# Layer 1 of a two-layer transformer: values, queries and keys by seven products of half blocks, with the residual kept in DRAM

## The chip, the core and the metric

The kernel runs on one core of a Trainium2 chip. The metric is the device time of one execution in microseconds (us). The engines are TensorE (PE; PEld is its weight load), VectorE (DVE), ScalarE (ACT), GpSimd (POOL) and SyncE (SP), which here issues DMA transfers. Everything is computed in float32. SBUF is the core's working memory of 128 partitions; PSUM holds matmul results in banks of 128 x 512 float32.

## What is computed

The input is x, 4 sequences of 512 tokens with 512 features. Both layers add attention and a mixture of experts to x. Layer 0 (sparse and windowed attention with 16 heads of 128, then experts) is not touched. Layer 1, cut to what matters:

```
xn = layernorm(x)
q, k, v = xn @ wq.T + bq,  xn @ wk.T + bk,  xn @ wv.T + bv        # 16 heads of 32
attn = softmax(q k^T / sqrt(32)) v ;  attn_out = attn @ wo.T + bo
top2 of 8 experts by xn @ router ;  h_e = silu(xn @ We + be)
combined = sum over the token's two experts of gate * h_e
y = xn + combined @ proj + b ;  ffn_out = norm_w * y / rms(y)
out = x + attn_out + ffn_out
```

## The kernel before

**Layout.** `acc` holds the residual, 16 tiles of 128 tokens x 512 features, in SBUF through the whole kernel. `xnT` is the normalised input, transposed: 4 blocks of 128 features, 2048 tokens (512 per sequence b). `xnd` is the same input by rows, in DRAM. The weights of layer 1 (`wqT`, `wkT`, `wvT`, `woT`) are 4 blocks of 128 input features x 512.

**Layer 1, groups and steps.** Its work is 16 groups g = (b, j), a sequence b and a block j of four heads. A group has four key chunks kc, so there are 64 steps. A step computes the scores of one key chunk for four heads (`weights`, matmuls at L996, exponentials on ACT at L998), and the products of the step before with the values (`attend`, L1010), with the sums of the exponentials kept on VectorE (L1016). Around that, the loop places: at kc 0 and 1 the next group's queries and keys (`queries`, L985, 8 matmul instructions of 512 columns into one PSUM bank, evicted with its bias by VectorE at L987); at kc 2 one of the four token tiles of the next sequence's values (`values`, L975, evicted at L977 with the bias `wv_b`); at kc 1 to 3 the division by the sums of the group before (`sum_keys` L1024, `invert` L1034, `scale_context` L1041); at kc 3 one output tile (`output1`, L1056), which `add_part` (L1047) adds to `acc`. A tile of the residual gets two additions, one from attention and one from the experts, and is stored to `out` after the second.

**The jobs beside it.** `schedule(jobs1)` hangs the mixture of experts on the same steps: routing in steps 0 to 9; 39 expert tiles, tile i in step 13 + 3i/4 (`fetch` loads 128 token rows, L379, and the expert's weights, L381, through POOL into two buffers; `turn` transposes the rows, L388; `apply` multiplies, L398, and evicts with bias and silu, L400 to L406); from step 44 on `mix`, `turn_mix` and `project_mix` of the 16 token tiles (L1081 to L1107), the last of which ends in the second kind of `add_part`. The fetch of tile i+2 is given out in the step of tile i and needs tile i's buffer.

**The order.** The program is written in this order of steps; a scheduler then orders the instructions on each engine by its own estimate, within the dependences. Each engine works its list in order. SP's list holds the DMA issues of stores to `out`, to `xnd` and `yd`, and of plain loads. In layer 1 one PSUM tag, "mm", with three banks serves queries, values, outputs, experts, transposes and sums.

**Between the layers.** `next_layer(n)` normalises tile n of the residual, and then POOL adds the output bias of layer 1 to it (L814, `acc[:, n, :] + wo_b`). The last four tiles are done while layer 1 begins: the first values, then the first queries, around 1480 to 1505 us. The loads of `wqT`, `wkT`, `woT` and `wv_b` are issued by SP at 1476.6 to 1479.7.

Of the kernel before, what the change touches and what calls it, by code (L numbers as in the profile page):

```python
# [44 lines left out]
def two_layers(ctx: ExitStack, tc: tile.TileContext, a: dict, out: bass.AP, large: bass.AP):  # L45
# [72 lines left out]
    yds = [dram.tile([NS * P, HID], F32, tag=f"yd{i}", name=f"yd{i}") for i in range(2)]  # L118

# [688 lines left out]
    def next_layer(n, pool, bank):  # L808
        make_rows, turn_ = layernorm(n, pool, bank)

        def rows():
            make_rows()

            G.tensor_tensor(acc[:, n, :], acc[:, n, :], rout["wo_b"], ALU.add)  # L814
        return rows, turn_
# [153 lines left out]

    def values(b, t):  # L970
        if t == 0:
            v[b] = ap_.tile([P, TC, HID], F32, tag="v", name=f"v1_{b}")
        vp = bank1("mm", f"vp_{b}_{t}")
        for k in range(KC):
            PE.matmul(vp, lhsT=xnT[:, k, ds(b * S + t * P, P)], rhs=wa["wvT"][:, k, :],  # L975
                      start=(k == 0), stop=(k == KC - 1))
        V.tensor_tensor(v[b][:, t, :], vp, rows["wv_b"], ALU.add)  # L977

    def queries(g, i):
        b, j = groups1[g]  # L980
        if i == 0:
            qk[g] = ap_.tile([P, 2, S], F32, tag="qk", name=f"qk_{g}")
        qp_ = bank1("mm", f"qp_{g}_{i}")
# [3 lines left out]
        V.tensor_scalar(qk[g][:, i, :], qp_, qkb[:, i, j : j + 1], None, ALU.add)  # L987

# [55 lines left out]
    left = {n: 2 for n in range(NT)}  # L1044

    def add_part(n, part_):
        V.tensor_tensor(acc[:, n, :], acc[:, n, :], part_, ALU.add)  # L1047
        left[n] -= 1
        if left[n] == 0:
            nc.sync.dma_start(out=out_v[n], in_=acc[:, n, :])  # L1050

    def output1(b, t):
# [5 lines left out]
        add_part(n, op)  # L1058
# [27 lines left out]
    def turn_mix(n):  # L1086
        g0, x = held[n]
        tr = bank1("mm", f"trc_{n}")
        for f in range(KC):
            PE.transpose(tr[:, ts(f, P)], g0[:, ts(f, P)], ident)  # L1090
        cT_ = rout["mix"].tile([P, KC, P], F32, tag="xT", name=f"combT_{n}")
# [4 lines left out]
    def project_mix(n):  # L1096
# [11 lines left out]
        add_part(n, y)  # L1108
# [22 lines left out]
    for n in range(NT):  # L1131
        here = first + n
        for d, f in ((0, mix), (1, turn_mix), (2, project_mix)):
            jobs1.append((at[min(here + d, len(at) - 1)], lambda n=n, f=f: f(n)))
    run1 = schedule(jobs1)
# [21 lines left out]
    for g in range(NG):  # L1157
        b, j = groups1[g]
        for kc in range(TC):
# [16 lines left out]
            if kc == 2 and b + 1 < B:  # L1176
                values(b + 1, j)

            if kc == 3 and g > NJ:
                output1(*divmod(g - NJ - 1, TC))  # L1180
            run1((g, kc))
    attend(*late)
# [703 lines left out]
```

## Time and profile before

| | us |
|---|---|
| time, median of 3 runs (lowest to highest) | 2130.55 (2126.63 to 2132.97) |
| the profiled execution: its time | 2132.48 |
| its span, first to last instruction | 2130.7 |
| its mean granted TensorE clock | 0.993 |
| TensorE busy in the span | 2076.4 (97%) |
| layer 1, from the first matmul of the values to the end | 1479 to 2130.7 |
| queries and keys in layer 1 (L985) | 1499 to 2056 |
| values (L975) | 1479 to 1950 |
| expert tiles (L398) | 1587 to 1917 |
| L985, one matmul instruction of 512 columns, first to last of it | 0.593 (they overlap) |
| L977 and L400, 128 x 512 from PSUM on VectorE | 0.69 |
| L1016, 128 x 1024 on VectorE | 1.22 |
| L381, expert weights: issue on POOL | 1.22 |
| L381, issue to landing, lowest, median, highest | 6.6, 8.9, 10.3 |

All views are of one execution. Its first part is the totals: busy time, share of the span and instructions of each engine. A table by stage gives busy time and number of instructions of each engine in a stretch from A to B us, then the granted clock (1 is full speed), the share of time that the 16 DMA engines were busy, and GB/s. The waits list who waited on what: total us, times, longest. A timeline row has start, duration, engine, line, operation, result and operands, number of instructions, and in brackets the idle time before it and what ended it. "x8" on TensorE is one group of four float32 matmuls, two instructions each.

### The profile page before, as it was taken

The page shows a single profiled execution, that of the slowest core. Times are in us where ns is not written, and L with a number is a line of the kernel's source. Part 1 is how long each engine was busy: PE and PEld are TensorE (multiplying, and loading weights), DVE is VectorE, ACT ScalarE, POOL GpSimd, SP SyncE. Part 2 cuts the span into 40 slices and gives each one's busy share as a digit, 9 for nine tenths or more (in the row PEclk, how much of TensorE's full clock was granted, in tenths as well). Part 3 has the DMA queues.
Part 4 walks back from the last instruction along what each step waited for, and adds up shares of the span by engine and source line. Part 5 has one row for each costly group of instructions (what it writes and reads, how often), then busy time and mean ns, then how long its engine had stood idle before and what let it go on. Part 6 is the DMA issues. An engine that isn't in the chain of part 4 may idle for free.

```text
span 2130.7 us, 27241 instructions
## 1 busy us (share of the span) xinstructions
PE 2076.4 (97%) x8946; PEld 1197.8 (56%) x8946; DVE 1431.2 (67%) x3436; ACT 867.5 (41%) x2649; POOL 686.7 (32%) x667
## 2 busy tenths in 40 slices
PE   7999999999999999999999999999999999999998
PEld 4566666666666666666666666664334343433333
DVE  7878867666666666666676687785575444546775
ACT  3444444444444344444444444443243233323332
POOL 3322244343232333232333344443012222213440
PEclk9999999999999999999999999999999999999998
DMA  7101134323433432443332222212026666653321
GB/s 253 72 30 58 40 101 129 129 90 116 144 104 121 134 99 94 135 125 112 116 126 99 90 70 70 75 50 94 16 98 224 224 211 206 212 168 124 104 85 41
DMA packets 84917, 244.53 MB, mean 115 GB/s; under 512 B 11424, under 2 KB 23712, under 8 KB 74784
## 3 DMA queue, kind: packets, MB, share of 16 engines
q0 software_dynamic: 22592, 139.47, 19.7%
q1 hardware_dynamic: 61024, 101.13, 14.6%
q10 hardware_dynamic: 1152, 2.10, 0.3%
q8 instruction: 74, 1.21, 0.2%
q14 instruction: 75, 0.61, 0.1%
HBM read 205.44 MB, written 37.22 MB: 114 GB/s over the span
## 4 chain that ended last, share of the span: by engine, by line
PE 66%; issue 13%; DVE 9%; POOL 5%; ACT 3%; DMA 3%; SPq 0%; POOLq 0%; ACTq 0%; DVEq 0%
PE p L534 21%; PE op L701 10%; PE hp_r L398 7%; PE st L626 4%; PE qp L985 3%; PE sp L617 2%; POOL we_r L381 2%; PE o L1056 2%; PE st L996 2%; PE ca L670 2%; ACT sq L438 1%; DMA we_r<-in_ewx,wrow_r 1%; PE vp L975 1%; PE cx L1010 1%; PE trq L554 1%
## 5 line engine op out<-in xcount | busy, mean ns | idle before, releaser
L398 PE MATMUL hp_r<-we_r,xT_r 128*128 128x512 f32 x624 | 285.1, 600 | 4.7 <-DMA we_r<-in_ewx,wrow_r 4.6
L379 POOL DMA_INDIRECT xr_r<-xnd,rows_r x78 | 93.1, 1194 | 483.6 <-PE trm_r L388 414.2
L701 PE MATMUL op<-Wo,cT 128*128 128x512 f32 x512 | 230.2, 598 | 4.5 <-DVE lv L598 3.1
L634 POOL TENSOR_TENSOR lT<-lT,lmask 128x512 f32<-128x512 f32 (+1 forms) x128 | 156.2, 1232 | 181.8 <-ACT lT L630 181.6
L398 PEld LDWEIGHTS hp_r<-we_r,xT_r 128*128 128x128 f32 x624 | 116.0, 192 | 140.9 <-issue 130.6
L534 PE MATMUL p<-wB,x 128*128 128x384 f32 x512 | 176.4, 488 | 4.1 <-DVE u L590 3.4
L534 PE MATMUL p<-wT,x 128*128 128x384 f32 x512 | 178.4, 491 | 0.3 <-DVE wT L106 0.3
L534 PE MATMUL p<-wA,xnT 128*128 128x384 f32 x512 | 174.0, 491 | 0.4 <-DVE u L569 0.4
L701 PEld LDWEIGHTS op<-Wo,cT 128*128 128x128 f32 x512 | 92.2, 190 | 114.0 <-issue 77.4
L438 ACT ACTIVATE sq<-qb 128x128 f32<-128x128 f32 x384 | 119.0, 310 | 88.7 <-DVE qb L583 35.3
L998 ACT ACTIVATE pT<-st 128x1024 f32<-128x1024 f32 x128 | 123.8, 1018 | 56.8 <-PE st L996 46.0
L390 ACT COPY xT_r<-trm_r 128x512 f32<-128x512 f32 x78 | 45.3, 581 | 230.7 <-PE trm_r L388 173.1
L704 DVE TENSOR_TENSOR acc<-acc,op 128x512 f32<-128x512 f32 x128 | 87.7, 685 | 72.9 <-PE op L701 72.6
L534 PEld LDWEIGHTS p<-wB,x 128*128 128x128 f32 x512 | 94.1, 191 | 67.3 <-issue 9.6
L534 PEld LDWEIGHTS p<-wT,x 128*128 128x128 f32 x512 | 94.9, 193 | 62.4 <-issue 8.0
L534 PEld LDWEIGHTS p<-wA,xnT 128*128 128x128 f32 x512 | 95.5, 193 | 60.0 <-DVE u L569 1.6
L548 ACT ACTIVATE qb<-qb,ss 128x128 f32<-128x128 f32 x256 | 81.9, 390 | 111.6 <-POOL ss L440 109.6
L630 ACT ACTIVATE lT<-st,ss 128x256 f32<-128x256 f32 (+1 forms) x128 | 46.8, 448 | 177.8 <-PE st L626 176.5
L400 DVE TENSOR_TENSOR yr_r<-hp_r,we_r 128x512 f32<-128x512 f32 x78 | 53.7, 688 | 92.9 <-PE hp_r L398 92.9
L413 POOL DMA_INDIRECT row_r<-yd,slot_r x64 | 73.4, 1147 | 119.1 <-DVE row_r L1082 53.0
L626 PE MATMUL st<-qkT 128*128 128x256 f32 (+1 forms) x512 | 109.3, 354 | 0.0
L626 PEld LDWEIGHTS st<-qkT 128*128 128x128 f32 x512 | 92.2, 191 | 10.8 <-issue 1.0
(262 smaller groups left out, 4204.2 us busy)
## 6 DMA issues: line engine op xcount, KB each, us to landing
x<-xsd SPq DMA_DIRECT2D x112, 256.0 KB, 3.0
yd<-yr_r SPq DMA_DIRECT2D x78, 256.0 KB, 2.6
wA<-in_wA SPq DMA_DIRECT2D x16, 384.0 KB, 4.0
wB<-in_wB SPq DMA_DIRECT2D x16, 384.0 KB, 8.3
xnd<-xn SPq DMA_DIRECT2D x24, 256.0 KB, 2.0
acc<-in_x SPq DMA_DIRECT2D x16, 256.0 KB, 5.1
Wo<-in_Wo SPq DMA_DIRECT2D x8, 512.0 KB, 3.7
xsd<-x SPq DMA_DIRECT2D x16, 256.0 KB, 2.0
```

The lines of the kernel that those rows point to most:

```text
L379: G.indirect_dma_start(out=x, out_offset=None, in_=xnd, in_offset=at_rows(self.r.rows[:, i : i + 1]))
L398: PE.matmul(hp, lhsT=xT[:, k, :], rhs=w[:, ts(k, HID)], start=(k == 0), stop=(k == KC - 1))
L413: G.indirect_dma_start(out=x, out_offset=None, in_=self.yd, in_offset=at_rows(self.r.slot[:, k, n : n + 1]))
L438: A.activation(sq, x[:, h, :], AF.Square, accum_out=ss[:, h : h + 1])
L534: PE.matmul(p, lhsT=x[:, k, ts(c, P)], rhs=w[:, k, :], start=(k == 0), stop=(k == 1))
L548: A.activation(x[:, j, :], x[:, j, :], AF.Copy, scale=sq[t][:, j : j + 1])
L626: PE.matmul(st[:, ds((t % 2) * 256, n)], lhsT=qkT[:, HG + h, ts(t, P)], rhs=qkT[:, h, ds(t * P, n)], start=True, stop=True)
L634: G.tensor_tensor(dst, dst, lmask.rearrange("p a w j -> p (a w j)")[:, 0:n], ALU.mult)
L701: PE.matmul(op, lhsT=cT[:, h, ts(t, P)], rhs=wo[:, h, :], start=(h == 0), stop=(h == HG - 1))
L704: V.tensor_tensor(acc[:, n, :], acc[:, n, :], op, ALU.add)
L985: PE.matmul(qp_, lhsT=wa[("wqT", "wkT")[i]][:, k, ts(j, P)], rhs=xnT[:, k, ts(b, S)], start=(k == 0), stop=(k == KC - 1))
L998: A.activation(pt[:, ts(pair, 2), :], st, AF.Exp, scale=SCALE1)
```

## The change

**Seven products.** A product of two 2 x 2 block matrices takes eight block products, or seven with sums of blocks formed before and after. For sequences 1 to 3 the change computes two things in this way. Queries and keys of a group (`queries7`): the weight side is [wq; wk] against the two halves of the features, the right side the two halves of the features against the two halves of the sequence. At kc 0 the products 1, 2, 6, 7 and at kc 1 the products 5, 4, 3, each of 2 feature blocks with 256 columns, two products to a bank. Values of a sequence (`values7`): four products (1, 2, 6, 7) at kc 2 and three (4, 5, 3) at kc 3 of the last group of the sequence before, each of four matmuls of 256 columns. Sequence 0 is computed as before.

**Sums.** The weight sums (`sums_qk` 4 operations of 128 x 1024, `sums_v` 4 of 128 x 512 and one of 128 x 256) are formed once, the sums of xnT (`sums_right`, 4 of 128 x 512) for each of sequences 1 to 3, all on VectorE; some overwrite a block of `wkT`, `wvT` or `xnT`, the others and the intermediate results lie in `acc`. Products are put together by VectorE, 9 operations per sequence for the values, and 3 at kc 0 and 4 at kc 1 for a group's queries and keys, with one copy on ACT.

**The residual.** For that, `acc` is given up in layer 1: `next_layer` stores each tile to `accd` in DRAM (SP), `bring` loads a tile before an addition into a place in sequence 0's part of `xnT` (or, for the last sequence, in `acc`), `add_part` adds there, and after the first of a tile's two additions it is stored again unless the other addition is going to use the same place.

```diff
+    accd = dram.tile([T, HID], F32, tag="accd", name="accd")
...
             G.tensor_tensor(acc[:, n, :], acc[:, n, :], rout["wo_b"], ALU.add)
+            nc.sync.dma_start(out=accd[ts(n, P), :], in_=acc[:, n, :])
...
+    two = lambda x: x.rearrange("p (k t) -> p k t", k=2)
+    sq1, sq2, sq4 = (acc[:, ts(n, 2), :] for n in range(3))
+    sv1, sv2, sv4, tx1, tx2, tx4 = (two(acc[:, n, :]) for n in range(6, 12))
+    us = [acc[:, n, :] for n in range(12, 15)]
+    f1, f2 = slice(0, 2), slice(2, 4)
+    h1, h2 = slice(0, 256), slice(256, 512)
+    def sums_left(a11, a12, a21, a22, s1, s2, s4):
+        return [lambda: V.tensor_tensor(s1, a21, a22, ALU.add), lambda: V.tensor_tensor(s2, s1, a11, ALU.subtract),
+                lambda: V.tensor_tensor(s4, a12, s2, ALU.subtract), lambda: V.tensor_tensor(a21, a11, a21, ALU.subtract)]
+    def sums_qk():
+        wq, wk_ = wa["wqT"], wa["wkT"]
+        return sums_left(wq[:, f1, :], wq[:, f2, :], wk_[:, f1, :], wk_[:, f2, :], sq1, sq2, sq4)
+    def sums_v():
+        w = wa["wvT"]
+        for f in sums_left(w[:, f1, h1], w[:, f2, h1], w[:, f1, h2], w[:, f2, h2], sv1, sv2, sv4):
+            f()
+        V.tensor_tensor(rows["wv_b"][:, h2], rows["wv_b"][:, h2], rows["wv_b"][:, h1], ALU.subtract)
+    def block(b, f, half):
+        return xnT[:, f, ds(b * S + half * 256, 256)]
+    def sums_right(b):
+        b11, b12, b21, b22 = (block(b, f, t) for f in (f1, f2) for t in range(2))
+        V.tensor_tensor(tx1, b12, b11, ALU.subtract)
+        V.tensor_tensor(b12, b22, b12, ALU.subtract)
+        V.tensor_tensor(tx2, b22, tx1, ALU.subtract)
+        V.tensor_tensor(tx4, tx2, b21, ALU.subtract)
     def values(b, t):
         if t == 0:
             v[b] = ap_.tile([P, TC, HID], F32, tag="v", name=f"v1_{b}")
...
                       start=(k == 0), stop=(k == KC - 1))
         V.tensor_tensor(v[b][:, t, :], vp, rows["wv_b"], ALU.add)
 
+    def values7(b, part_):
+        w = wa["wvT"]
+        u1, u2, u3 = (two(u) for u in us)
+        bias = [rows["wv_b"][:, h].unsqueeze(1).to_broadcast([P, 2, 256]) for h in (h1, h2)]
+        def product(nm, left, right):
+            p = two(bank1("mm", f"v{nm}_{b}"))
+            for c in range(2):
+                for k in range(2):
+                    PE.matmul(p[:, c, :], lhsT=right[:, k, ts(c, P)], rhs=left[:, k, :], start=(k == 0), stop=(k == 1))
+            return p
+        if part_ == 0:
+            v[b] = ap_.tile([P, TC, HID], F32, tag="v", name=f"v1_{b}")
+            V.tensor_tensor(u1, product("p1", w[:, f1, h1], block(b, f1, 0)), bias[0], ALU.add)
+            V.tensor_tensor(v[b][:, 0:2, h1], product("p2", w[:, f2, h1], block(b, f2, 0)), u1, ALU.add)
+            V.tensor_tensor(u2, product("p6", sv2, tx2), u1, ALU.add)
+            V.tensor_tensor(u3, product("p7", w[:, f1, h2], block(b, f1, 1)), u2, ALU.add)
+            V.tensor_tensor(u3, u3, bias[1], ALU.add)
+        else:
+            V.tensor_tensor(v[b][:, 0:2, h2], u3, product("p4", w[:, f2, h2], tx4), ALU.subtract)
+            p5 = product("p5", sv1, tx1)
+            V.tensor_tensor(u2, p5, u2, ALU.add)
+            V.tensor_tensor(v[b][:, 2:4, h2], p5, u3, ALU.add)
+            V.tensor_tensor(v[b][:, 2:4, h1], product("p3", sv4, block(b, f2, 1)), u2, ALU.add)
     def queries(g, i):
         b, j = groups1[g]
         if i == 0:
             qk[g] = ap_.tile([P, 2, S], F32, tag="qk", name=f"qk_{g}")
+        if b:
+            return queries7(g, i)
         qp_ = bank1("mm", f"qp_{g}_{i}")
         for k in range(KC):
             PE.matmul(qp_, lhsT=wa[("wqT", "wkT")[i]][:, k, ts(j, P)], rhs=xnT[:, k, ts(b, S)],
                       start=(k == 0), stop=(k == KC - 1))
         V.tensor_scalar(qk[g][:, i, :], qp_, qkb[:, i, j : j + 1], None, ALU.add)
+    def queries7(g, part_):
+        b, j = groups1[g]
+        wq, wk_ = wa["wqT"], wa["wkT"]
+        u1, u2, u3 = (u[:, ts(g % 2, 256)] for u in us)
+        bq, bk = (qkb[:, n, j : j + 1] for n in range(2))
+        q, key = qk[g][:, 0, :], qk[g][:, 1, :]
+        def products(nm, *pairs):
+            p = bank1("mm", f"q{nm}_{g}")
+            for n, (left, right) in enumerate(pairs):
+                for k in range(2):
+                    PE.matmul(p[:, ts(n, 256)], lhsT=left[:, k, ts(j, P)], rhs=right[:, k, :], start=(k == 0), stop=(k == 1))
+            return p[:, h1], p[:, h2]
+        if part_ == 0:
+            p1, p2 = products("p12", (wq[:, f1, :], block(b, f1, 0)), (wq[:, f2, :], block(b, f2, 0)))
+            A.copy(u1, p1)
+            V.scalar_tensor_tensor(q[:, h1], p2, bq, u1, ALU.add, ALU.add)
+            p6, p7 = products("p67", (sq2, tx2), (wk_[:, f1, :], block(b, f1, 1)))
+            V.tensor_tensor(u2, p6, u1, ALU.add)
+            V.tensor_tensor(u3, p7, u2, ALU.add)
+        else:
+            p5, p4 = products("p54", (sq1, tx1), (wk_[:, f2, :], tx4))
+            V.tensor_tensor(u2, p5, u2, ALU.add)
+            V.scalar_tensor_tensor(key[:, h2], p5, bk, u3, ALU.add, ALU.add)
+            V.scalar_tensor_tensor(key[:, h1], u3, bk, p4, ALU.add, ALU.subtract)
+            p3, _ = products("p3", (sq4, block(b, f2, 1)))
+            V.scalar_tensor_tensor(q[:, h2], p3, bq, u2, ALU.add, ALU.add)
 
     def weights(g, kc):
 
...
         V.tensor_reduce(ends[:, 0, g : g + 1], rs, AX.X, ALU.max)
 
     left = {n: 2 for n in range(NT)}
-
-    def add_part(n, part_):
-        V.tensor_tensor(acc[:, n, :], acc[:, n, :], part_, ALU.add)
+    lies = {}
+    def bring(n, way):
+        if (n, 1 - way) in lies:
+            lies[n, way] = lies[n, 1 - way]
+            return
+        if n < NT - TC:
+            lies[n, way] = xnT[:, way * 2 + n % 2, 0:S]
+        elif left[n] == 2:
+            lies[n, 0] = lies[n, 1] = acc[:, 2 * NT - TC - 1 - n, :]
+        nc.sync.dma_start(out=lies[n, way], in_=accd[ts(n, P), :])
+    def add_part(n, part_, way):
+        x = lies.pop((n, way))
+        V.tensor_tensor(x, x, part_, ALU.add)
         left[n] -= 1
         if left[n] == 0:
-            nc.sync.dma_start(out=out_v[n], in_=acc[:, n, :])
+            nc.sync.dma_start(out=out_v[n], in_=x)
+        elif (n, 1 - way) not in lies:
+            nc.sync.dma_start(out=accd[ts(n, P), :], in_=x)
 
     def output1(b, t):
         n = b * TC + t
...
         for jj in range(NJ):
             PE.matmul(op, lhsT=cT1[b][:, jj, ts(t, P)], rhs=wa["woT"][:, jj, :],
                       start=(jj == 0), stop=(jj == NJ - 1))
-        add_part(n, op)
+        add_part(n, op, 0)
 
     r1 = Routing("r1", lg1, rp, const, bank1)
     held = {}
...
         tr = bank1("mm", f"trc_{n}")
         for f in range(KC):
             PE.transpose(tr[:, ts(f, P)], g0[:, ts(f, P)], ident)
+        bring(n, 1)
         cT_ = rout["mix"].tile([P, KC, P], F32, tag="xT", name=f"combT_{n}")
 
         A.activation(cT_, tr.rearrange("p (k t) -> p k t", k=KC), AF.Copy, scale=0.5)
...
         V.tensor_scalar(ss, ss, 1.0 / HID, 1e-6, ALU.mult, ALU.add)
         G.tensor_tensor(ss, ss, nhalf[:, 0:1], ALU.pow)
         V.scalar_tensor_tensor(y, y, ss[:, 0:1], rows["nw1"], ALU.mult, ALU.mult)
-        add_part(n, y)
+        add_part(n, y, 1)
 
 
     at = [(g, kc) for g in range(NG) for kc in range(TC)]
...
         here = first + n
         for d, f in ((0, mix), (1, turn_mix), (2, project_mix)):
             jobs1.append((at[min(here + d, len(at) - 1)], lambda n=n, f=f: f(n)))
+    left_ = sums_qk()
+    for place, f in (((1, 1), left_[0]), ((1, 2), left_[1]), ((1, 3), left_[2]), ((2, 0), sums_v), ((2, 1), left_[3])):
+        jobs1.append((place, f))
+    for b in range(1, B):
+        jobs1.append(((b * NJ - 2, 2), lambda b=b: sums_right(b)))
     run1 = schedule(jobs1)
 
     values(0, 0)
...
                     scale_context(g - 1)
             if kc < 2 and g + 1 < NG:
                 queries(g + 1, kc)
-            if kc == 2 and b + 1 < B:
-                values(b + 1, j)
-
+            if kc > 1 and j + 1 == NJ and b + 1 < B:
+                values7(b + 1, kc - 2)
+            if kc == 1 and g > NJ:
+                bring(g - NJ - 1, 0)
             if kc == 3 and g > NJ:
                 output1(*divmod(g - NJ - 1, TC))
             run1((g, kc))
+        if g + 1 == NG:
+            bring(NT - TC - 1, 0)
     attend(*late)
     sum_keys(NG - 1)
     output1(B - 2, TC - 1)
```

## The prediction

> **What bounds the kernel now.** The changed stretch is layer 1 of the profiled execution, 1479 us to the end at 2130.7. I read the page's totals first, then the table by stage, then the waits, and last the timelines of single steps. Totals:
>
> ```profile
> span 2130.7 us, 27241 instructions
> ...
> PE 2076.4 (97%) x8946; PEld 1197.8 (56%) x8946; DVE 1431.2 (67%) x3436; ACT 867.5 (41%) x2649; POOL 686.7 (32%) x667
> ```
>
> TensorE is the bound on the whole: whoever saves TensorE work saves time, unless TensorE then waits for something else. The table by stage (columns: PE, PEld, DVE, ACT, POOL busy; granted clock; DMA share; GB/s) tells where it would:
>
> ```profile
> 1516.00:1573.00 57.00, 56.83 (x299) 20.18 (x298) 52.00 (x109) 23.01 (x29) 4.42 (x4) 1.00 0.04 9
> 1600.00:1900.00 300.00, 295.87 (x1081) 121.19 (x1079) 137.52 (x170) 95.66 (x141) 74.89 (x69) 0.99 0.63 213
> 2000.00:2060.00 60.00, 57.06 (x226) 22.99 (x225) 42.32 (x58) 20.25 (x36) 27.78 (x26) 1.00 0.36 105
> 2050.00:2061.00 11.00, 10.80 (x41) 4.41 (x40) 10.51 (x13) 0.60 (x1) 4.25 (x3) 1.00 0.32 90
> 2060.00:2131.00 71.00, 59.35 (x204) 22.20 (x202) 40.38 (x62) 18.68 (x31) 8.93 (x9) 0.90 0.13 42
> ```
>
> Four regimes. From 1516 to 1573 VectorE is nearly as full as TensorE, 52 of 57 us (routing, sums over keys, reciprocals). In the 300 us of the experts TensorE stands 4.1 us in all, VectorE is under half busy and the DMA engines move 213 GB/s. In the mixing stage TensorE has 2.9 us of 60 free while VectorE fills single steps (2050 to 2061: 10.51 of 11), and in the tail 11.7 of 71. So in the expert stage TensorE looks like the sole bound. The waits in layer 1 (total, times, longest) and the landing times of the expert weights say that a second loop runs just beside it:
>
> ```profile
> POOL we_r L381 <- DVE yr_r L400: 65.0, 10, 9.0
> ...
> PE hp_r L398 <- DMA we_r<-in_ewx,wrow_r: 4.6, 4, 2.2
> ```
> ```profile
> DMA to landing us min/median/max: 6.6/8.9/10.3
> ```
>
> The weights have two buffers. POOL issues the load for expert i+2 only when VectorE has evicted expert i, and it lands 8.9 us later. One turn of that loop, on TensorE:
>
> ```profile
> 1677.14 3.60 PE L398 MATMUL hp_r<-we_r,xT_r 128*128 128x512 f32 x8
> ...
> 1683.61 3.70 PE L975 MATMUL vp<-wvT,xnT 128*128 128x512 f32 x8
> 1687.15 3.60 PE L398 MATMUL hp_r<-we_r,xT_r 128*128 128x512 f32 x8
> ...
> 1691.73 3.70 PE L398 MATMUL hp_r<-we_r,xT_r 128*128 128x512 f32 x8
> ```
> ```profile
> 1682.70 1.22 POOL L381 DMA_INDIRECT we_r<-in_ewx,wrow_r  x1 [0.30 <-issue]
> ```
>
> Expert 11's products end at 1680.7, its eviction at 1681.5, POOL issues the load of 13 at 1682.70, it lands at 1691.5, and 13 starts at 1691.73: TensorE's work between them (transposes 1.0, weights and attend 2.1, vp 3.5, expert 12's products 3.5, weights 1.1: 11.2) just fills the loop. The same stands before experts 5, 9, 17, 21, 25, 29, 33 and 37 (0.1 to 1.1 us between landing and start). Experts 18 and 34, whose landing the trace lacks, have 0.6 to 0.7 by their issue and 8.9. For most others the slack is 2 to 7 us. Work taken from TensorE inside such a turn comes back as a wait.
>
> **The change part by part.** A group of four 512-column matmuls (8 instructions) takes 3.54 us from start to start above (1683.61 to 1687.15), 3.43 where groups of one kind follow each other: 0.86 per matmul. In layer 0, 16 instructions of 384 columns took 5.17 us (L534), 0.32 each against 0.43: columns set the cost, and a half-block product (4 matmuls of 256) costs 1.72.
>
> **TensorE's own saving.** Queries and keys: 12 groups x (8 - 7) x 0.86 = 10.3 us, all at key chunk 1 (6 matmuls of 256, 2.58, for 3.43; chunk 0 stays 3.44). Values: 3 sequences x (4 x 3.43 - 7 x 1.72) = 5.1. Together 15.4 us, 0.7%. This is what the change can gain at most.
>
> **Values, moved.** I number the steps 4g + kc. Before, one vp of 3.5 us stood in steps 2, 6, 10, ..., 46. After, only the last group before each sequence has them: 4 products (6.87) in steps 14, 30, 46 and 3 (5.16) in 15, 31, 47. What leaving the others out is worth:
>
> Steps 2, 6, 10 (1524 to 1570) are VectorE-bound. VectorE loses three evictions (2.1 us) and gains one sum of weights that cannot be earlier (left_[3], 1.2; it overwrites wkT). Gain at least 2.1 - 1.2 = 0.9, at most the 57 - 51.1 = 5.9 to its busy time, of 10.6 removed. I take 3.
>
> Steps 22, 26, 34, 38 lie inside turns like the one shown (experts 11 to 13, 16 to 18, 27 to 29, 32 to 34). With vp gone from the turn above, TensorE comes to expert 13 at 1688.2 and its weights at 1691.5: 0.1 of 3.5 is left. The other turns have slack 0.6 to 0.7 and give that: 0.1 + 0.7 + 0.6 + 0.6 = 2.0 of 14.1. Bounds 0 and 14.1.
>
> Step 18 (a turn with slack) and step 42 (after the last expert) give 3.5 each, 7.0.
>
> Added are 3 x (6.87 - 3.53) + 3 x 5.16 = 25.5, of which 0.9 is absorbed by the wait before an expert of step 31: 24.6.
>
> Net 3 + 2.0 + 7.0 - 24.6 = -12.6 (a loss), between -17.6 (0.9 and 0 in the first two, nothing absorbed) and +2.4. The new sums of the products on VectorE (9 x 0.69 per sequence for 4 x 0.69) run in a stage where it is under half busy, beside the next product, with three banks to rotate; uncovered they would cost at most 3.4 per sequence. I count them below.
>
> **Queries.** Of the 12 savings of 0.86, eight fall at steps 13 to 41 and four at 45 to 57. In the first eight some are in turns without slack, and the expert's eviction in a chunk-1 step now stands behind four small additions: I take 4.9 of 6.9, bounds 0 and 6.9. In the last four VectorE sets the step:
>
> ```profile
> 2054.66 2.49 DVE L1016 TENSOR_TENSOR pS<-pT,pT 128x1024 f32<-128x1024 f32 x1
> 2057.08 0.94 DVE L1034 RECIPROCAL rsum<-rsum 128x128 f32<-128x128 f32 x1
> 2057.94 0.65 DVE L987 TENSOR_SCALAR qk<-qp,qkb 128x512 f32<-128x512 f32 x1
> 2058.51 1.75 DVE L1034 RECIPROCAL rsum<-rsum 128x128 f32<-128x128 f32 x2
> ```
>
> VectorE works without a gap from 2051.5 to 2062, and in such a step one 0.65 eviction becomes four of 128x256. No row has that size: 128x128 took 0.22 and 128x512 0.69, I take 0.42, so 1.7 for 0.65, +1.0 (bounds +0.2 and +2.1). Four steps of which some three are like this, less a little saved: -1.5, bounds -6 and +3.4. The ACT copy of p1 (0.31 to 0.58 by its rows) and three small additions at chunk 0 (+0.5) lie beside weights and attend: nothing; if that cover is gone, another 0.5 x 12.
>
> **The hand-over at 1480.** SP's queue and the first eviction of the values:
>
> ```profile
> 1478.13 0.43 SPq L776 DMA_DIRECT2D wkT<-in_wkT  x1
> 1478.61 1.03 SPq L776 DMA_DIRECT2D woT<-in_woT  x1
> 1479.69 0.68 SPq L72 DMA_DIRECT2D wv_b<-in_wv_b  x1
> ```
> ```profile
> 1489.25 1.29 DVE L977 TENSOR_TENSOR v<-vp,wv_b 128x512 f32<-128x512 f32 x2 [5.05 <-DMA wv_b<-in_wv_b]
> ```
>
> The twelfth store of the residual to DRAM is put before these loads on SP and waits for POOL's addition of wo_b (1477.8 to 1479.1): wkT, woT and wv_b go 1.4 to 2.1 us later. On VectorE three sums of query and key weights (3 x 1.16 by L1016) stand before the values' eviction: wkT at about 1487.3, sums to 1490.8, wv_b at 1491.2, eviction at about 1492 and not 1489.25. TensorE fills three banks and waits: -3, bounds -1 and -5. The other sums (4 x 0.69 of wvT and three times 4 x 0.69 of xnT) are issued before 1480, or in the under-half-busy expert stage: nothing, with the tail of layer 0 as cover (at most 1.4).
>
> **DRAM traffic.** 16 stores and some 30 loads and stores of 0.26 MB. The loads go out a group ahead, where a load of such rows (xnd to xa) landed in 2.8 us; but on SP the load of xa and the stores of y now stand behind stores that wait for additions, and POOL already waits 9.9 us for xa in 4 mixes. I take -2 for these and the exposed value sums, bounds 0 and -8.
>
> Sum: -12.6 + 4.9 - 1.5 - 3 - 2 = -14.2: 2132.5 + 14.2 = 2146.7 for the profiled execution (span 2130.7 and 1.8 around it). It lies 1.9 above the median of the runs shown, so **2144.8** is the forecast.
>
> One rule speaks against taking fillers out. Rows first: in the tail, with 11.7 us of 71 idle, the granted clock was 0.90; from 2000 to 2060, with 2.9 of 60 idle in pieces, 1.00. By these rows new waits of up to 3.4 us, scattered, leave the clock alone, and the sum above stands. The Trainium skill, TensorE: Matmul & The Clock Gate (Part 1: The HAM clock gate), says that the clock is halved once TensorE has been idle for a window of some 3.4 us. By it, as an estimate, four waits that just crossed that window would each run 3.4 us at half speed and lose 1.7, and the sum would be some 7 us worse.
>
> **The rivals.** Three.
>
> **Faster**, ending below 2124.2. TensorE stays the sole bound: expert weights land in time however little TensorE has to do. Then the values lose nothing in the four turns: +12.1, and 1516 to 1573 gives its 5.9: +2.9; queries 6.9: +2; the mixing steps hold (+3.5), hand-over -1: +2, traffic 0: +2. -14.2 + 24.5 = 10.3 gained, 2120.3. It decides when the loads take 5.4 us rather than 8.9; the fastest seen was 6.6. For it: TensorE 97% busy everywhere. Against: eight starts within 1.1 us of their landing. Chance 0.11.
>
> **The same**, 2124.2 to 2137.0. The loop gives way by half, the weights landing some 1.5 us sooner (7.4) in four turns: +6, and the hand-over costs 1 and not 3: +2. -6.2, 2136.8. 0.14.
>
> **Much slower.** In the mixing stage the loads of xa stand on SP behind stores whose additions come later on VectorE by the four additions of a chunk-1 step (1.7 to 2.2). If six of the 16 mixes are late by 2.2: 13 us more, 2158. For it: POOL's wait for xa and the gapless VectorE. Against: TensorE has other steps' work in hand. 0.10.
>
> My forecast has 0.65. That the change saves no TensorE work at all I leave out: fewer columns are multiplied, and columns set the cost.
>
> **How the numbers follow.** 0.3% of 2130.6, about what a measurement tells from no change, is 6.4. Faster 0.11, same 0.14, slower 0.65 + 0.10 = 0.75. The bad bounds of single terms give 2147 to 2151, two together up to 2156; the good bound of the values alone gives 2129.8, and rival 1 lies at 2120. The range 2129 to 2157 leaves out most of rival 1 (0.1) and of rival 3 (0.08). The forecast's own range is 2137 to 2155.
>
> **What the profile after would show.** Right: TensorE's busy time falls by some 15 us while the waits of hp_r for we_r grow from 4.6 to 12 us or more; 1516 to 1573 shrinks by 3 only; first v eviction near 1492; mixing steps no shorter. Wrong: waits for we_r as before (rival 1), the landing of we_r well under 8.9 (rival 2), or POOL waiting tens of us for xa (rival 3). The sum would be off most if the turns are not what holds steps 22, 26, 34 and 38.

## The result, and the profile after

The changed kernel takes 2143.42 us (median of 5 runs, 2141.29 to 2146.24) against 2129.48 before (also 5 runs, 2126.63 to 2132.97): a ratio of 1.0065, 95% interval 1.005 to 1.008. It is 13.9 us slower, although it multiplies fewer columns. The forecast was 2144.8, some 14 us slower. The profiled execution of the changed kernel stands 10.9 us above that of before (spans 2141.6 and 2130.7).

The totals on the page of the changed kernel:

```profile
span 2141.6 us, 27924 instructions
...
PE 2069.0 (97%) x9162; PEld 1239.1 (58%) x9162; DVE 1469.0 (69%) x3532; ACT 873.4 (41%) x2661; POOL 691.2 (32%) x667
```

TensorE is still busy for 97%. Its busy time fell by 7.4 us and not by 15; but busy time is no count of work (its ends are modelled, and a matmul at a lower clock is busy for longer): the kernel below whose values are only moved, with the same products as before, is busy for 2078.8, which is 2.4 us more. The timelines show the saving group by group.

The waits in layer 1 of the changed kernel (total, times, longest), and the landing times of the expert weights:

```profile
POOL we_r L383 <- DVE yr_r L402: 76.2, 12, 11.1
...
PE hp_r L400 <- DMA we_r<-in_ewx,wrow_r: 10.7, 7, 3.2
```
```profile
DMA to landing us min/median/max: 6.7/8.8/10.6
```

TensorE waits 10.7 us for expert weights where it waited 4.6, though they land as fast as before (8.8 against 8.9 us). This is the turn that the prediction showed, from expert 11 to expert 13, now without a group of the values in it; first TensorE, then POOL's issue:

```profile
1678.97 3.60 PE L400 MATMUL hp_r<-we_r,xT_r 128*128 128x512 f32 x8
...
1685.43 3.70 PE L400 MATMUL hp_r<-we_r,xT_r 128*128 128x512 f32 x8
1689.06 1.12 PE L1094 MATMUL st<-qk 32*128 32x512 f32 x2
1693.39 3.99 PE L400 MATMUL hp_r<-we_r,xT_r 128*128 128x512 f32 x5 [3.21 <-DMA we_r<-in_ewx,wrow_r]
```
```profile
1684.52 1.23 POOL L383 DMA_INDIRECT we_r<-in_ewx,wrow_r  x1 [0.30 <-DMA we_r<-in_ewx,wrow_r]
```

From the start of expert 11 to the start of expert 13 it was 14.59 us (1677.14 to 1691.73) and is 14.42 (1678.97 to 1693.39). 3.5 us of products left, and 3.21 came back as a wait in front of expert 13. (The view of TensorE ends at 1697, so its last row holds five of expert 13's eight instructions.) The reader should look at that row's bracket: the releaser is the DMA. Its issue at 1684.52 hangs on expert 11's eviction as before: the eviction ends at 1683.37 (1681.47 before), POOL issues the load of the token rows at 1683.27 (1681.45), and the weights follow 1.25 us behind in both. The bracket of POOL's row names another landing, that of expert 12 at 1684.27, but it is expert 11's buffer that the load fills.

The hand-over, on SP and on VectorE:

```profile
1480.30 0.32 SPq L817 DMA_DIRECT2D accd<-acc  x1
1480.67 0.48 SPq L778 DMA_DIRECT2D wkT<-in_wkT  x1
1481.20 0.67 SPq L778 DMA_DIRECT2D woT<-in_woT  x1
1481.91 0.74 SPq L72 DMA_DIRECT2D wv_b<-in_wv_b  x1
```
```profile
1487.34 1.23 DVE L985 TENSOR_TENSOR acc<-wkT 128x1024 f32<-128x1024 f32 x1 [0.76 <-DMA wkT<-in_wkT]
1488.60 1.23 DVE L985 TENSOR_TENSOR acc<-acc,wqT 128x1024 f32<-128x1024 f32 x1
1489.86 1.23 DVE L986 TENSOR_TENSOR acc<-wqT,acc 128x1024 f32<-128x1024 f32 x1
1491.35 1.29 DVE L1018 TENSOR_TENSOR v<-vp,wv_b 128x512 f32<-128x512 f32 x2 [0.27 <-DMA wv_b<-in_wv_b]
```

The store of the residual stands ahead of wkT, woT and wv_b on SP, whose issue is 2.2 to 2.6 us later than before, and three sums of weights stand ahead of the first eviction of the values, which starts at 1491.35 and not at 1489.25 (the forecast said 1492). But the first matmul of the values starts at 1480.31 here and at 1479.12 before, so 1.2 us of each of these differences stands ahead of layer 1.

For where the time goes I compare the start of each step in the two traces (the step's first exponential on ACT), the changed kernel less the one before:

| step | 0 | 3 | 8 | 12 | 16 | 19 | 24 | 28 | 32 | 40 | 43 | 48 | 63 | end |
|---|---|---|---|---|---|---|---|---|---|---|---|---|---|---|
| us | +1.2 | -2.3 | +0.8 | -2.5 | +7.7 | +3.4 | +3.2 | +1.1 | +8.4 | +5.7 | -1.3 | +11.8 | +12.0 | +11.0 |

The three clusters of the values (steps 14 to 15, 30 to 31, 46 to 47) put the time in; between them it comes back only in part. The +1.2 at step 0 is what stands ahead of layer 1: from the first matmul of the values to step 0 both traces take 30.59 us.

### The profile page after: what moved, and what is told of

Same layout as the page of the kernel before. It is cut to its first block, busy times and chain, and to the rows that moved or that the text cites. A ratio compares the mean times of both kernels' runs of the same rounds, so it can differ in the third digit from the quotient of the medians.

```text
span 2141.6 us, 27924 instructions
## 1 busy us (share of the span) xinstructions
PE 2069.0 (97%) x9162; PEld 1239.1 (58%) x9162; DVE 1469.0 (69%) x3532; ACT 873.4 (41%) x2661; POOL 691.2 (32%) x667
## 4 chain that ended last, share of the span: by engine, by line
PE 70%; DVE 12%; issue 6%; DMA 4%; ACT 4%; POOL 3%; SPq 0%; ACTq 0%; POOLq 0%; DVEq 0%
PE p L536 21%; PE hp_r L400 10%; PE op L703 10%; PE st L628 4%; PE sp L619 2%; DMA we_r<-in_ewx,wrow_r 2%; PE o L1170 2%; PE st L1094 2%; PE qp L1070 2%; DVE pS L1114 2%; ACT sq L440 2%; PE ca L672 2%; PE vp L1030 1%; PE trm_r L390 1%; PE cx L1108 1%
## 5 line engine op out<-in xcount | busy, mean ns | idle before, releaser
L400 PE MATMUL hp_r<-we_r,xT_r 128*128 128x512 f32 x624 | 285.5, 601 | 10.7 <-DMA we_r<-in_ewx,wrow_r 10.7
L1094 PE MATMUL st<-qk 32*128 32x512 f32 x512 | 96.0, 659 | 5.4 <-ACT pT L1096 5.3
```

Source lines behind the costliest of these rows:

```text
L400: PE.matmul(hp, lhsT=xT[:, k, :], rhs=w[:, ts(k, HID)], start=(k == 0), stop=(k == KC - 1))
L1094: PE.matmul(st[:, i, :], lhsT=qk[g][rows_, 1, ts(kc, P)], rhs=qk[g][rows_, 0, :], start=True, stop=True)
```

## The experiments

All ratios are against the kernel before, run beside them: its median was 2129.5 beside the change and 2130.0 to 2131.4 beside the others.

| kernel | us, median | ratio, 95% interval |
|---|---|---|
| the change | 2143.4 | 1.0065 (1.005 to 1.008) |
| values moved only | 2146.3 | 1.0081 (1.0063 to 1.0099) |
| values by seven products only | 2147.5 | 1.0090 (1.0073 to 1.0107) |
| queries and keys by seven products only | 2126.3 | 0.9981 (0.9972 to 0.9991) |
| the same for sequences 1 and 2 only | 2129.5 | 0.9992 (0.9983 to 1.0002) |
| residual in DRAM only | 2132.3 | 1.0011 (1.0001 to 1.0020) |
| values' seven products spread, sums in time | 2130.5 | 0.9998 (0.9989 to 1.0008) |
| residual in DRAM, three weight buffers | 2124.3 | 0.9968 (0.9958 to 0.9979) |
| values moved, three buffers | 2131.7 | 1.0005 (0.9995 to 1.0015) |
| values by seven products, three buffers | 2130.8 | 0.9997 (0.9987 to 1.0006) |
| queries by seven products, three buffers | 2117.2 | 0.9934 (0.9918 to 0.9951) |

### The place alone

```diff
-            if kc == 2 and b + 1 < B:
-                values(b + 1, j)
+            if kc > 1 and j + 1 == NJ and b + 1 < B:
+                for t in range(2):
+                    values(b + 1, 2 * kc - 4 + t)
```

> The kernel before with nothing changed but the place of the values of sequences 1 to 3: plain products, two token tiles at kc 2 and two at kc 3 of the last group of the sequence before, no sums, residual in SBUF. My theory (the place costs): the four fillers of 3.5 us per sequence go, of which some 13 us in all come back as shorter steps, and 3 x (3.4 + 6.9) - 0.9 = 30 us are added; about +16 us, 2145 against 2129.5. Rival (TensorE's work alone counts, so the place is indifferent, and products, sums or DRAM traffic make the change slow): within 3 us of before.

Measured: 2146.33, 15.6 us above before. No product, sum or DMA differs from the kernel before; only the place of nine groups does. It costs as much as the whole change (the intervals of the two overlap). In its trace TensorE's wait for the weights grows from 4.6 to 8.7 us:

```profile
PE hp_r L398 <- DMA we_r<-in_ewx,wrow_r: 8.7, 6, 3.5
```

### Queries and keys alone, values alone, the round trip alone

Queries and keys by seven products, values plain in their four places, in an order that the sums of xnT allow, and no sums of the values' weights:

```diff
-            if kc > 1 and j + 1 == NJ and b + 1 < B:
-                values7(b + 1, kc - 2)
+            if kc == 2 and b + 1 < B:
+                values(b + 1, (j + 2) % TC)
...
```

> The changed kernel with the values of sequences 1 to 3 as before (plain, one token tile at kc 2 of each group, in the order 2, 3, 0, 1 because the sums of xnT overwrite a block); queries and keys by seven products, residual in DRAM. My theory: the loss through the values goes (12.6 us), the rest stays: 2143.4 - 12.6 = 2131, between 2127 and 2132. Rival (seven products of queries or the DRAM traffic cost the time): 2138 or more.

Measured: 2126.27, 4.4 us faster than before. So the values carry the loss: without their change the kernel is 17 to 18 us faster than the changed one (17.15 between the medians, 17.0 between the spans, 18.4 if each is taken against the kernel before beside it), more than the 12.6 forecast.

Values by seven products, queries and keys plain (with one block of sums in a place of its own, so that xnT stays whole):

```diff
-        if b:
-            return queries7(g, i)
...
-        V.tensor_tensor(b12, b22, b12, ALU.subtract)
+        V.tensor_tensor(tx3, b22, b12, ALU.subtract)
...
```

> The changed kernel with plain queries and keys; values by seven products in the last group, residual in DRAM, sums of the values' weights and of xnT kept (one more place for a block of sums). My theory: 2129.5 + 12.6 + 1 to 3 for hand-over and traffic = 2143 to 2146, so about what the whole change costs. Rival (queries are the cost): 2132 or less.

Measured: 2147.46. It is 1.1 us from the plain values in the same places, within the intervals of the two: the saving of 5.1 us on TensorE left no mark in the total. (This kernel also keeps the residual in DRAM, which costs 1.6 by itself as the next run shows; that does not make up the 5.1.)

The round trip, with plain products everywhere and no sums:

```diff
-        if b:
-            return queries7(g, i)
...
-    left_ = sums_qk()
...
-    for b in range(1, B):
-        jobs1.append(((b * NJ - 2, 2), lambda b=b: sums_right(b)))
...
```

> The kernel before with the residual of layer 1 in DRAM (stores after POOL's addition, loads before each addition) and nothing else: no products, no sums. My theory: 1.2 us at the hand-over through the store ahead of the weights on SP, and up to 2 in the mixing stage: 2130 to 2133. Rival (the DRAM traffic on SP's queue makes the change slow): 2138 or more.

Measured: 2132.30, ratio 1.0011: 1.6 us above the median of before. 14.2 MB more (258.7 for 244.5) through the DMA engines and SP's queue are nearly free. Against this kernel the seven products of queries and keys gain 6.0 us (2126.3).

### A third buffer for the expert weights

In the kernels with the residual in DRAM, part of `acc` is free while the experts run. Every third expert tile is loaded there, so that the load of tile i+2 no longer waits for the eviction of tile i:

```diff
-            w = self.pool.tile([P, (KC + 1) * HID], F32, tag="we", name=f"we_{self.r.name}_{i}", bufs=bufs)
+            if self.silu and i % 3 == 2:
+                w = acc[:, 11:16, :].rearrange("p k t -> p (k t)")
+            else:
+                w = self.pool.tile([P, (KC + 1) * HID], F32, tag="we", name=f"we_{self.r.name}_{i}", bufs=bufs)
...
```

> The kernel before with the residual in DRAM as in the run of the round trip alone (2132.3), and a third buffer for the expert weights in the freed acc (every third expert tile), so that the load of tile i+2 no longer waits for the eviction of tile i. Base for the next runs. My theory: the waits of hp_r for we_r (4 us) go, 2127 to 2131. Rival (the weights' loads are bound by transfer, not by the buffer): unchanged, 2132, with the same waits.

Measured: 2124.29, 8.0 below the round trip alone, more than expected. The wait of TensorE for the weights is gone from the trace altogether, while they land as slowly as ever; here is the view of the tile of the weights:

```profile
DMA to landing us min/median/max: 6.8/9.1/10.2
```

So it was the buffer that bound the loads, not the transfer. Against the trace of the round trip alone step 19 is 4.6 us shorter: a wait of 2.90 us in front of expert 9 is gone, and with it a lowered clock behind it (see the clock, below). The same with the values moved:

> The same with plain values in the last group, two tiles at kc 2 and two at kc 3. With two buffers the move cost 15.6 us. My theory: of the 31 us of vacated products the loop over two buffers ate most of those in steps 22 to 38; with three buffers all six after step 17 come back (21) and some 5 of the three before: the move costs about 5, so 5 above the run with the third buffer alone. Rival (not the loop; the vacated steps are held by something else, or the added steps are dearer than their products): 13 to 16 above it.

Measured: 2131.67, 7.4 above the run with the third buffer alone, against 15.6 with two buffers. The step starts of the two traces show it: with three buffers the steps 18, 22, 26, 34 and 38 give 3.43 us back each and step 42 3.21. With two, steps 22 and 34 gave nothing (they lost 0.5 and 1.9 us) and 26 and 38 gave 2.5 and 2.9. With three buffers the added steps of the first two clusters cost their products and no more, 3.43 and 6.87. The loop is thereby shown to be what ate the vacated steps.

Values by seven products in those places:

> Values by seven products in the last group, plain queries and keys, residual in DRAM, three buffers for the expert weights. Plain values in the same places with three buffers took 2131.7. My theory: the vacated steps give their time back as there, and of the 5.1 us less on TensorE some stays, less 1 at the hand-over and some 4 in steps 46 to 48, where the trace of the changed kernel shows TensorE waiting for VectorE to free banks: 2129 to 2133. Rival (the loop was not the cause, values by seven products are slow in themselves): 2140 or more.

Measured: 2130.78. Without the loop the saving of the seven products is seen: against the plain values in the same places each of the first two clusters is 1.6 to 1.7 us shorter (1.72 by the sum). The third is not: from step 46 to 48 this trace loses 3.2 us. There TensorE waits 2.33 us for an eviction, and the clock is at 0.50 for 3.4 us behind it. The rest of the kernel loses 4.3 more in this trace, but it is that of the slowest of ten runs (2135.86); the medians differ by 0.9, in favour of the seven products and within the noise.

Queries and keys by seven products, plain values, three buffers:

> Queries and keys by seven products, plain values in their four places, residual in DRAM, three buffers for the expert weights. With two buffers 2126.3, and the trace gave none of the 6 us saved in steps 13 to 40. My theory: they come back, with the waits for we_r: 2117 to 2122. Rival (VectorE's additions hold those steps): 2125 to 2128.

Measured: 2117.19, ratio 0.9934: 14 us faster than before (10 to 17 by the interval), and the fastest of all kernels here. The table by stage, of the queries' kernel with two buffers and then with three (PE, PEld, DVE, ACT and POOL busy, clock, DMA share, GB/s):

```profile
1600.00:1900.00 300.00, 295.20 (x1162) 137.43 (x1161) 147.68 (x204) 98.35 (x148) 73.28 (x69) 0.99 0.66 224
```
```profile
1600.00:1900.00 300.00, 300.00 (x1204) 140.25 (x1203) 151.60 (x209) 101.90 (x154) 73.19 (x68) 1.00 0.66 225
```

TensorE stands 4.8 us of 300 in the first and never in the second, with the same traffic. By the step starts, the eight savings of the queries' seven products in steps 13 to 41 gained 0.5 us with two buffers (against the round trip alone), and 2.8 us with three (against the third buffer alone). That is not the whole 6.9: in steps 17, 21, 29 and 33 the 0.84 is seen each time and in step 41 0.77, but at steps 13, 25 and 37 the order of the expert tile against the queries shifts, so that the step is 4.73 us shorter and the next 5.13 longer, a loss of 0.4 each in place of a gain of 0.84. These eight are the same with two buffers; there step 31 is 2.1 us longer besides, where the wait for expert 25's weights is 1.43 us (1.00 in the round trip alone) and the clock is halved behind it. What makes the three dearer was not tried, nor was the whole change, values included, with three buffers.

### The values' products spread over four groups

Products 1 and 2 at kc 2 of the first group, 3 of the second, 6 and 7 of the third, 5 and 4 of the fourth:

```diff
-            if kc > 1 and j + 1 == NJ and b + 1 < B:
-                values7(b + 1, kc - 2)
+            if kc == 2 and b + 1 < B:
+                values7(b + 1, j)
...
```

> The changed kernel with the seven products of the values spread over kc 2 of the four groups: products 1 and 2; 3; 6 and 7; 5 and 4 (intermediate results in the tile of the values itself, 10 operations on VectorE for 9); two buffers for the weights. My theory: the place was the cost; with fillers back in every group it is near the run with plain values (2126.3), from 2123 to 2130. Rival (the products of the values themselves are dear: VectorE's operations, sums, banks): 2135 to 2143.

Measured: 2131.52. In this kernel product 3 of sequence 1 read the sums of the weights before they were formed, the work being the same. With the sums in time:

> As the run before with the values' products spread over kc 2 of four groups (1 and 2; 3; 6 and 7; 5 and 4), with the sums of the values' weights formed four steps earlier, before product 3 of sequence 1 uses them. There the time was 2131.5. My theory as it stands after that run: the place gives back most of the 17 us that the clustered values cost over plain ones, but with two weight buffers the saving of 5 us on TensorE does not come back and VectorE's additional operations cost a few: 2127 to 2132. Rival (the products themselves are as dear as their cluster): 2138 or more.

Measured: 2130.46, the same as before the change (0.9998). The same seven products, spread out, take 13 us less than in a cluster; so they are not dear in themselves. But with two buffers they are no gain either: plain values in one group each, at the same key chunk, took 2126.3.

### Which queries gain

> Queries and keys by seven products for sequences 1 and 2 alone, plain for sequence 3, whose queries lie in the mixing stage (steps 45 to 57); plain values in their places, residual in DRAM, two weight buffers. With sequence 3 as well it was 2126.3, with none 2132.3. By my prediction the seven products of sequence 3 lose 1.5 and this kernel takes some 2125. By the traces of those two runs (no gain in steps 13 to 40, several us after 45) it is sequence 3 that gains: 2129 to 2132.

```diff
-        if b:
+        if b in (1, 2):
             return queries7(g, i)
...
```

Measured: 2129.52, 3.2 above the kernel in which sequence 3 has seven products too (1 to 5 by the scatter of the runs). So sequence 3, whose queries lie in the mixing stage, gains some 3 us: my prediction, which had it lose 1.5, is wrong there. The step starts agree: from step 45 to 58 sequence 3's products gain 3.1 us in this pair of traces, 2.9 against the round trip alone, and 2.3 in the pair with three buffers.

## Why the prediction was right, point by point

The mechanism, that vacated steps do not come back beside a second loop while added ones cost their full price, is what the runs show. But the total (13.9 for 14.2) is closer than its parts, and that is luck: the values cost 17 and not 12.6, the queries gained 6.0 and not 3.4, the hand-over and the DRAM traffic cost some 2 and not 5. Of the signs I had named, the waits for the weights stopped at 10.7 (I said 12 or more), and TensorE's busy time fell by half of what I said.

The values' term by stretches, from the starts of the steps (the changed kernel less the one with seven products for queries only; plus is a loss):

| steps | 0 to 13 | 14, 15 | 16 to 29 | 30, 31 | 32 to 43 | 44 to 47 | 48 to end | sum |
|---|---|---|---|---|---|---|---|---|
| forecast, us | -3 | +8.5 | -4.3 | +7.6 | -4.7 | +8.5 | 0 | +12.6 |
| measured, us | -2.5 | +8.7 | -5.6 | +5.5 | -4.8 | +12.7 | +1.5 | +15.4 |

In steps 30 and 31 the queries' kernel itself has the 2.1 us of step 31 named above; against the kernel before, the stretch costs 7.8.

**The loop over the weights' two buffers: right in kind, and in two of four turns in size.** The prediction gave 2.0 of 14.1 us back in steps 22, 26, 34 and 38. The move alone, run with two and with three buffers (15.6 and 7.4 us), shows that the loop decides this. By the step starts of the changed kernel against the one with seven products for queries only, the four steps gave -1.4, +2.6, +0.1 and +2.5 us: 3.7 in all. Steps 26 and 38 gave more than the 0.6 to 0.7 that I read from issue and 8.9 us: expert 18's weights were issued at 1730.1 and its products began at 1737.04, so they landed within 6.9 us. That is the mechanism of the second rival, and it held in two of four turns.

**Steps 2, 6 and 10: right in size, in part by luck.** Forecast 3 us, of a bound of 5.9; up to step 13 the trace shows 2.5. But steps 2, 6 and 10 gave 8.4 us by themselves (3.4, 1.6 and 3.4), and 3.6 went again in step 7, over which the clock is halved, as shown below. The prediction had held VectorE alone responsible.

**The added steps: right for two clusters, too small for the third.** Steps 14 and 15 together grew by 8.65 us for 8.5. In that cluster the products run as priced, 1.73 us from start to start:

```profile
1609.66 1.99 PE L1030 MATMUL vp<-wvT,acc 128*128 128x256 f32 x8
1611.49 1.89 PE L1030 MATMUL vp<-acc 128*128 128x256 f32 x8
1613.22 1.89 PE L1030 MATMUL vp<-acc,xnT 128*128 128x256 f32 x8
1614.95 3.60 PE L400 MATMUL hp_r<-we_r,xT_r 128*128 128x512 f32 x8
```

The step that failed is "run in a stage where it is under half busy, beside the next product, with three banks to rotate". This holds in the expert stage, but the third cluster lies in steps 46 and 47, in the mixing stage. There, first TensorE and then VectorE:

```profile
1944.01 3.72 PE L1030 MATMUL vp<-wvT,xnT 128*128 128x256 f32 x16 [0.64 <-DVE qk L1083]
1947.57 1.89 PE L1030 MATMUL vp<-acc 128*128 128x256 f32 x8
1951.05 1.99 PE L1030 MATMUL vp<-wvT,xnT 128*128 128x256 f32 x8 [1.59 <-DVE acc L1034]
1952.88 3.60 PE L1215 MATMUL po<-pw,combT 128*128 128x512 f32 x8
```
```profile
1948.52 0.74 DVE L1196 SCALAR_TENSOR_TENSOR row_r<-row_r,gate_r,row_r 128x512 f32<-128x512 f32 x1
1949.18 1.21 DVE L1114 TENSOR_TENSOR pS<-pS,pT 128x1024 f32<-128x1024 f32 x1
1950.32 0.68 DVE L1034 TENSOR_TENSOR acc<-vp,wv_b 128x512 f32<-128x512 f32 x1
1950.92 0.93 DVE L1132 RECIPROCAL rsum<-rsum 128x128 f32<-128x128 f32 x1
1951.78 0.62 DVE L1035 TENSOR_TENSOR v<-vp,acc 128x512 f32<-128x512 f32 x1
```

Two products run at 1944.01, a third at 1947.57, and then the banks are full: VectorE is among the sums of the keys, the gates and the reciprocals, evicts the first product only at 1950.32, and TensorE waits 1.59 us. From step 44 to 48 the kernel lost 12.7 us against the one with plain values, for 8.5 priced; waits for banks, 0.64 and 1.59, make 2.2 of the 4.2. The two traces are 1.6 us apart at step 0 already, and little of that is the values': 1.3 stands at 300 us, in layer 0, where the two programs are the same. The sums of the values' weights do cost something: behind the first of them (1435.79 on VectorE) TensorE falls 0.5 us behind the trace of before, and in the kernel without these sums it does not. The prediction put them at nothing, with 1.4 as the bound.

**Queries: too little, and both parts wrong.** I gave 4.9 in the expert stage and -1.5 in the mixing stage, 3.4 in all. Measured against the round trip they gained 6.0: 0.5 up to step 41, and the rest behind it, some 3 of it through sequence 3. In the expert stage I gave 4.9 of 6.9; with three buffers 2.8 came, so the loop took 2.3, and the rest went into the three shifts of order named above, of which I had thought only as the eviction behind four additions. In the mixing stage "VectorE sets the step" was the step that failed. VectorE did get its additional work (in 2000 to 2060 it was busy 45.9 us with seven products for sequence 3 and 42.4 without), and still the kernel gained. My reading, which no run tests by itself, is that a gapless VectorE in an 11 us stretch isn't yet the bound of the stage: the same 60 us hold steps where it has room, and the 0.86 saved on TensorE counts there. Here are the two table rows, first without and then with seven products for sequence 3 (the 0.97 of the first holds a stretch of 3.4 us at half the clock; the second trace has its own just ahead of the window, at 1996.6, and from step 45 to 58 each has one, so the clock does not make the gain):

```profile
2000.00:2060.00 60.00, 57.04 (x222) 22.76 (x221) 42.43 (x60) 19.71 (x34) 28.03 (x25) 0.97 0.46 140
```
```profile
2000.00:2060.00 60.00, 58.10 (x265) 27.76 (x267) 45.93 (x75) 21.83 (x39) 27.96 (x24) 1.00 0.49 149
```

**Hand-over and DRAM: too dear.** I gave 3 and 2. Counted from the first matmul of the values the first eviction is 0.9 us later and step 0 not at all (30.59 us in both traces). "TensorE fills three banks and waits" is what failed: in both traces it runs two groups of the values, the router's products (3.6 us), a transpose and a third group in the same time, and none of them waits for the eviction. The 1.2 us at step 0 come from layer 0: 0.5 stands there from 100 us on, where the programs are the same, and 0.5 comes with the sums named above. The round trip in all costs 1.6. My third rival, loads of xa held up on SP, did not come in its size: POOL's wait for xa rose from 9.9 us to 16.1, and to 14.3 in the kernel with the round trip alone.

**The rivals.** "Faster" fell for the reason that was held against it, and its condition could be made: with loads that need not wait for an eviction, the kernel with seven products for the queries ends at 2117. Its sum had a slip: with the mixing steps at +3.4 in place of -1.5 the term is 4.9 and not 3.5, and its time 2118.9. "The same" was right on two turns of four.

## The clock

The rule weighed in the prediction turned out to matter, and my reading of the rows, that waits of up to 3.4 us leave the clock alone, was wrong. The changed kernel around step 7 (TensorE busy, its granted clock, DMA share, GB/s), and TensorE's timeline there:

```profile
1540.00:1545.00 5.00, 3.66 (x27) 1.00 0.02 3
1545.00:1550.00 5.00, 4.27 (x16) 0.64 0.00 0
1550.00:1555.00 5.00, 5.00 (x30) 0.67 0.00 2
1555.00:1560.00 5.00, 5.00 (x31) 1.00 0.00 0
```
```profile
1542.21 1.07 PE L1108 MATMUL cx<-pT,v 128*32 128x512 f32 x8
1543.21 0.46 PE L359 MATMUL tp_r<-mark_i_r,mark_r_r 128*128 128x78 bf16 x8
1545.73 2.99 PE L1094 MATMUL st<-qk 32*128 32x512 f32 x8 [2.07 <-ACT pT L1096]
1548.65 1.94 PE L1108 MATMUL cx<-pT,v 128*32 128x512 f32 x8
```

Behind a wait of 2.07 us the granted clock is 0.50 for 6.8 us, from 1546.4 to 1553.3 (the 0.64 and 0.67 above are means over 5 us), and eight score matmuls take 2.99 us where they take 1.14. Step 7 takes 3.6 us longer than before: as much as one of the three groups taken from this stretch. The four other kernels with the values in one group, moved or by seven products, have a wait of 2.06 or 2.07 us at the same place, and behind it the clock is 0.50 for 3.4 or 6.8 us; the kernel before has neither there. It has such a place elsewhere, behind a wait for weights:

```profile
1655.46 5.30 PE L398 MATMUL hp_r<-we_r,xT_r 128*128 128x512 f32 x8 [2.24 <-DMA we_r<-in_ewx,wrow_r]
```

There 2.24 us of waiting made an expert's products take 5.30 and not 3.60. The same happened behind expert 13 in the turn above (clock 0.50 from 1693.4 to 1696) and behind expert 29 after 1.98 us. In the traces of layer 1 every such stretch that the end of the kernel does not cut short lasts 3.4 or 6.8 us. The Trainium skill, TensorE: Matmul & The Clock Gate (Part 1: The HAM clock gate), puts the window of idleness at some 3.4 us, free-running. The length agrees with these stretches, and the prediction's estimate from it, 1.7 us for a crossing, with 5.30 less 3.60. As a bound on one wait it doesn't hold: here waits of 2.07 and 2.24 us were enough, while another of 2.31 us (ahead of expert 8 in the changed kernel, at 1654.21) was followed by the full clock, and expert 8's products took 3.67. What decides between them was not tried.

## What to carry to other kernels

Before taking work from the busiest engine, look for the loops that run just beside it: a load that waits for an eviction of two tiles ago, lands after 9 us and is then used at once is a second bound, and what is saved within its turn can come back as a wait, up to the whole of it (3.21 of 3.5 us in front of expert 13). The place of filler work counts as much as its amount: nine plain groups moved to other steps cost 15.6 us without any change of the work. And when memory is freed, look first whether the loop beside the bound can use it: a third buffer was worth 8 us, and with it the queries' smaller products gained 2.8 us in the expert stage, for 0.5 without it.

## What was not expected of the hardware

A wait of TensorE of 2.07 us was followed by 6.8 us at half the clock, one of 2.31 us by none, and the stretches at half the clock last 3.4 or 6.8 us. The expert weights landed no faster in the changed kernel (8.8 against 8.9 us), nor with a third buffer (9.1).
